# Vision tower on one core: the q, k and v projections as seven products of quarters

## The chip, the cores and the metric

The kernel runs on one core of one Trainium2 chip. The metric is the device time of one execution in microseconds (us). Before the change it is 2117.93 us, the median of three runs from 2116.43 to 2118.93. The engines are named as in the profile: PE multiplies matrices (PEld is its loading of the stationary operand), DVE and ACT work element by element, POOL does small arithmetic and issues indirect transfers, SP issues most of the other transfers.

## The reference

The input x is cut into overlapping patches of 16 samples, each is Fourier transformed, and a matrix W maps the result to tokens of 256 features. On these tokens h stand two residual layers: a retention layer with an MLP, and a mixture of eight experts of which each token uses two.

```python
h = tokens(x) @ W.T
# layer 0, on t = layernorm(h)
a = layernorm(t)
q, k, v = a @ Wq.T + bq, a @ Wk.T + bk, a @ Wv.T + bv
mem = 0
for each token: mem = decay * mem + k * v ; ret = q * mem
t = t + ret
h = h + t + relu(layernorm(t) @ W1.T + b1) @ W2.T + b2
# experts, on u = layernorm(h)
h = h + u + sum over the two chosen e of  weight[e] * (gelu(u @ w1[e] + b1[e]) @ w2[e] + b2[e])
```

There are 16384 tokens, in 32 blocks of 512. All arithmetic that matters here is in 32 bits.

## The kernel before

**Blocks.** The 32 blocks of 512 tokens go through the stages in a software pipeline. In pass `i` of the main loop (0 to 30) the block `new = blocks[i]` is embedded, normalised and sent through q, k, v and the retention scan; `mid = blocks[i-1]` goes through the MLP; `old = blocks[i-2]` is routed to the experts. After the loop the last block (31), the MLP of block 30 and the remaining expert tiles are done in an order written out by hand.

**Expert tiles.** A routed token is written by an indirect transfer to a buffer `xbuf` in its expert's rows. Whenever 256 rows of an expert are full they make a *tile*: `load` fetches weights, rows (turned by the transfer) and shares; `turn` joins the halves on ACT; `enter` does the first product and the Gelu; `leave` the second product; `sums` scales the result on DVE and adds it to the output by an indirect transfer. `slot()` fits one tile step into the pass if more than three tiles are in hand; there are four slots in a pass: after the embedding, after the fourth MLP product group, ahead of the first half of `mlp_out` and ahead of its second half. `take` finds with some twenty small DVE operations which tiles became full.

**Order of work.** The instruction streams of PE, DVE, ACT and SP keep the order of the program (`manual_schedule`); POOL's are placed by the framework. In each pass the order on PE is: five embedding products (L378), a slot, the first MLP layer `mlp_in` (eight groups, L321 with `w_sb`) with a slot after the fourth, the router products `logits` (L583), q, k, v for both halves of the features (L321 with `wqkv_sb`), the counting products of `place` (L653), a slot, `mlp_out(0)` (L517), the transposes of `residual` (L476), a slot, `mlp_out(1)`.

**q, k, v.** `retention(m)` makes for each half m of the 256 features three products of the 512 tokens by 256 features, each as two accumulated matrix products of 512 columns, in one PSUM bank from the pool `p_mm` (four banks). ACT adds the bias of k, DVE adds that of v and multiplies by k, a scan on DVE runs the memory, and DVE adds q's bias and multiplies. On PE each product in 32 bits is two instructions, so a block has 24 of them.

**Transposition of the features.** For blocks 6 to 30 the normalised tokens `zz` are split by ACT into 16-bit planes, turned by a transfer (`turned<-planes`, issued by SP at L309) and joined by DVE (`features1`, L315, for q, k, v) or by ACT (`features2`, for the MLP). The single buffer `turned` also serves the router's turn of the tokens (`turn3`, joined by DVE in `join3`). For blocks 0 to 5 and 31 PE turns them (L288).

**DVE's order in a pass**, as far as it matters: `retention` and `choose` (the routing, which ends in the tile `both`), `place`, `take`, the tile's `sums`, the add and statistics of `mlp_out(0)`, `residual` with its norm, `sums`, the add and statistics of `mlp_out(1)`, the norm's apply (which waits for POOL's `rstd`), the embedding's combinations, its norms, `sums`, `join3`, `sums`, the first part of the next block's `differences`, the join of hT, the second part.

PSUM has eight banks: four in `p_mm`, three in `p_tm` (embedding, transposes, second products) and one in `p_sm` (router and counting products).

Of the kernel before, what the change touches and what calls it, by code (L numbers as in the profile page):

```python
# [36 lines left out]
def vit_tower_kernel(  # L37
# [24 lines left out]
    G = P // TT  # L62
    BLK = TT * P
    U = TT // 2
    NV = 8
# [25 lines left out]

    p_mm = ctx.enter_context(tc.tile_pool(name="p_mm", bufs=4, space=bass.MemoryType.PSUM))
    p_tm = ctx.enter_context(tc.tile_pool(name="p_tm", bufs=3, space=bass.MemoryType.PSUM))
    p_sm = ctx.enter_context(tc.tile_pool(name="p_sm", bufs=1, space=bass.MemoryType.PSUM))
    ident = const.tile([P, P], F32)
# [56 lines left out]
    wqkv_sb = const.tile([P, 3, KD, D], F32)  # L152
    nc.sync.dma_start(out=wqkv_sb, in_=wqkv.rearrange("w (k p) d -> p w k d", p=P))
    w1_sb = const.tile([P, KD, H], F32)
    nc.sync.dma_start(out=w1_sb, in_=w1.rearrange("(k p) h -> p k h", p=P))
# [57 lines left out]
    def fold(w, g, b, to, room, ps):  # L213
# [21 lines left out]
        for k in range(KD):  # L235
            nc.scalar.mul(w[:, :, k, :], w[:, :, k, :], vec[:, g + k : g + k + 1])

    class Norm:

# [76 lines left out]

    def feature_mm(w, rhs, m):

        ps = p_mm.tile([P, BLK], F32, name="mm")
        for k in range(KD):  # L320
            nc.tensor.matmul(ps, lhsT=w[:, k, ts(m, P)], rhs=rhs[:, k, :], start=k == 0, stop=k == KD - 1)  # L321
        return ps
# [9 lines left out]
    class Block:  # L332
# [93 lines left out]
        def retention(self, m):  # L426

            if m == 0:
                self.kv = one.tile([P, KD, BLK], F32, name="kv")
                self.ret = one.tile([P, KD, BLK], F32, name="ret")  # L430
            ks = two.tile([P, BLK], F32, name="ks")
            at = slice(m, m + 1)

            def tiles_order(a):
                return a.rearrange("p (r w) -> p w r", r=TT)

            def own_order(a):
                return a.rearrange("p (w r) -> p w r", r=TT)

            pk = feature_mm(wqkv_sb[:, 1], self.hT, m)  # L440
            nc.scalar.activation(own_order(ks), tiles_order(pk), AF.Identity, bias=vec[:, BK + m : BK + m + 1])  # L441
            pv = feature_mm(wqkv_sb[:, 2], self.hT, m)
            nc.vector.scalar_tensor_tensor(
                own_order(self.kv[:, m, :]),
                tiles_order(pv),
                vec[:, BV + m : BV + m + 1],
                own_order(ks),
                ALU.add,
                ALU.mult,
            )  # L450
            nc.vector.tensor_tensor_scan(  # L451
                ks,
                vec[:, DEC + m : DEC + m + 1].to_broadcast([P, BLK]),
                self.kv[:, m, :],
                0.0 if self.i % NBLK == 0 else carry[:, at],
                ALU.mult,
                ALU.add,
            )
            nc.vector.tensor_copy(carry[:, at], ks[:, BLK - 1 : BLK])
            pq = feature_mm(wqkv_sb[:, 0], self.hT, m)  # L460
            nc.vector.scalar_tensor_tensor(
                tiles_order(self.ret[:, m, :]),
                tiles_order(pq),
                vec[:, BQ + m : BQ + m + 1],
                own_order(ks),
                ALU.add,
                ALU.mult,
            )

        def residual(self):  # L470
            norm = Norm()
            for u in range(U):
# [7 lines left out]
                for i in range(2):  # L480
                    norm.stats(self.z, 2 * u + i)
            norm.factors_here()
            self.zz = one.tile([P, TT, D], F32, name="zz")
# [19 lines left out]
        def mlp_in(self, m):  # L503
            if m == 0:
                self.aT = one.tile([P, KH, BLK], F32, name="aT")
            ps = feature_mm(w1_sb, self.hT, m)
            nc.scalar.activation(self.aT[:, m, :], ps, AF.Relu, bias=vec[:, MB1 + m : MB1 + m + 1])  # L507

        def mlp_out(self, u, between=None):
            if u == 0:  # L510
                self.norm = Norm()
            ps = p_tm.tile([P, 2, D], F32, name="tm")
            for i in range(2):
                if i and between:
                    between()
                for k in range(KH):
# [10 lines left out]
            if u == U - 1:  # L527
                self.norm.factors_here() if self.i >= NS - 1 else self.norm.factors()
                self.tok = one.tile([P, TT, D], F32, name="tok")
                self.norm.apply(self.tok, self.h)  # L530
                if self.i == NS:
                    nc.vector.tensor_tensor(self.h, self.h, self.tok, ALU.add)
                    return
                mean, rstd = self.norm.mv[:, :, 0], self.norm.rstd[:, 0, :]
                self.by = small.tile([P, 2, TT], F32, name="by")
                nc.vector.tensor_scalar(self.by[:, 0, :], rstd, 1.0, None, ALU.add)
                nc.vector.scalar_tensor_tensor(self.by[:, 1, :], mean, -1.0, rstd, ALU.mult, ALU.mult)

        def store(self):
# [38 lines left out]
        def logits(self):  # L578
            self.lg = p_sm.tile([P, TT, G], F32, name="sm")
            for k in range(KD):  # L580
# [67 lines left out]
        def place(self, at_once=True):  # L648

            oh = self.oh  # L650
            ps = p_sm.tile([P, 2, TT, E], F32, name="sm")
            for i in range(2):
# [62 lines left out]
    def take(n, block, writes):  # L715
# [23 lines left out]
        shape = [P, k, E]  # L739
        past = small.tile([P, KMAX, E], F32, name="past")[:, :k, :]  # L740
        nc.vector.tensor_tensor(
# [272 lines left out]

    def slot(known, load=True):

        if len(tiles) - at["enter"] > LEFT and at["enter"] + 2 <= known:
            expert_step(load=load)

# [6 lines left out]
    with tc.manual_schedule(engines=MANUAL):  # L1026
# [3 lines left out]
        for i in range(NS):  # L1030
# [5 lines left out]
            next(embed)  # L1036
            if at["enter"] == 0:
                advance("turn", 2)
            if i > 1:
# [15 lines left out]
            next(embed, None)  # L1055
            slot(known, load=False)
            if old:
                old.join3()
            for m in range(KH):
                if mid:  # L1060
                    mid.mlp_in(m)
                if m == 1:
                    new.split1()

                    if at["enter"]:
                        advance("load", at["enter"] + AHEAD - 1)
                if m == TT - 1:
                    slot(known)
                if m == KH // 2 and old:
                    old.store()  # L1070
                if m == KH - 3:
                    ahead = blocks[i + 1].differences(xs.pop(i + 1))
                    next(ahead)
                    new.features1()
                    next(ahead)
            if i == NS - 1:
                slot(known)
            if old:
                old.logits()
            for m in range(KD):  # L1080
                new.retention(m)
                if old and m == 0:
                    old.choose()
            if old:
                take(old.i + 1, old, old.place(at_once=False))
                old.scatter(1)
            if i + 2 < NB:
                xs[i + 2] = load_x(i + 2)
            slot(known)
            if old:  # L1090
                old.scatter(2, last_product[0])
            if mid:
                mid.mlp_out(0)
            if old:
                old.scatter(3, last_product[0])
            new.residual()
            slot(known, load=False)
            if old:
                old.scatter(4, last_product[0])
            if at["enter"] == 0:  # L1100

                advance("load", 2)
            if i:
                new.split2()
            if at["enter"]:
                advance("load", at["enter"] + AHEAD - 1)
            if mid:
                mid.mlp_out(1)

# [14 lines left out]
        for m in range(KH):  # L1124
# [5 lines left out]
            if m == KH - 3:  # L1130
                last.features1()
        next(weights)
        old.logits()
# [3 lines left out]
        next(weights)  # L1137
        last.retention(0)
        mid.mlp_out(0)
        next(weights)  # L1140
        take(NS - 1, old, writes)
        next(weights)
        mid.mlp_out(1)
        last.retention(1)
        beside = expert_halves(fetch=False)
        next(beside)
        mid.features3()
        mid.rows()
        advance("leave", at["enter"] - 1)
        mid.logits()  # L1150
        mid.choose()
        run(beside)
        expert_step(fetch=False, sums=False)
        writes = mid.place()
        advance("sums", at["leave"])
        expert_step(fetch=False, sums=False)
        last.residual()
        expert_step(fetch=False, sums=False)
        advance("sums", at["leave"])
        expert_step(fetch=False)  # L1160
        take(NS, mid, writes)
# [17 lines left out]
        del tiles[at["load"] :]  # L1179
        cuts = [0] + [min(len(rest), len(rest) * e // (E - 1) + 0) for e in range(1, E)] + [len(rest)]  # L1180
        for e in range(E):
            tiles.extend(rest[cuts[e] : cuts[e + 1]])
            tiles.append(Expert(e, last))
# [99 lines left out]
```

## Time and profile before

The profiled execution took 2119.29 us, with a span of 2117.5 us from its first to its last instruction and a mean granted PE clock of 0.997.

| group | count | busy us | mean ns |
|---|---|---|---|
| PE, second MLP product, L517, 256 columns | 2048 | 453.3 | 380 |
| PE, first MLP product, L321, 512 columns | 1024 | 450.3 | 592 |
| PE, q, k, v products, L321, 512 columns | 768 | 339.0 | 598 |
| PE, embedding products, L378, 256 columns | 1280 | 282.5 | 379 |
| PE, tile products, L859 and L876, 256 columns | 1048 each | 251.6 and 249.5 | 383 and 381 |
| DVE, h add of the MLP, L524 | 64 | 44.2 | 690 |
| DVE, scan, L451 | 56 | 71.9 | 1284 |
| DVE, ret, L461 | 64 | 70.6 | 1104 |
| ACT, bias of k, L441 | 64 | 44.0 | 687 |
| ACT, Gelu, L867, 256 columns | 262 | 109.5 | 470 |
| ACT, copy of embedding products, L387, 512 columns | 32 | 18.7 | 585 |

The mean of a PE instruction is longer than the step from one to the next, because instructions overlap: busy time by count gives the step. A block's lines in a timeline (start and duration in us, engine, line, operation, output and inputs, and in brackets the idle time ahead of it and what ended it) show the order of the work; DVE, ACT and POOL each do one instruction at a time in order.

### The profile page before, as it was taken

What the parts mean: (1) busy time and instruction counts of PE and PEld (TensorE: products, weight loads), DVE (VectorE), ACT (ScalarE), POOL (GpSimd) and SP (SyncE); (2) the same over time, 40 slices, a digit from 0 to 9 for tenths busy, and PEclk for the clock granted to TensorE, in tenths of its full rate; (3) what the DMA queues carried; (4) which work ended last, traced back from release to release, by engine and by line L of the source; (5) the groups of instructions that cost most, each with busy time, mean ns of one, the idle gap of its engine ahead of it and who ended that gap; (6) DMA issues with size and microseconds to landing.
All of it is one profiled execution on the core that took longest, in us unless ns stands there. A gap on an engine that the chain in (4) does not pass through costs nothing.

```text
span 2117.5 us, 28820 instructions
## 1 busy us (share of the span) xinstructions
PE 2093.3 (99%) x8502; PEld 1478.1 (70%) x8502; DVE 1653.6 (78%) x5176; ACT 832.4 (39%) x1329; POOL 876.4 (41%) x769
## 2 busy tenths in 40 slices
PE   8999999999999999999999999999999999999989
PEld 6666666677776667777666777666677766677766
DVE  7778877878888788888878888787788888777545
ACT  2222334444334444433444433344443334443533
POOL 1122243344444444444434444433444443355444
PEclk9999999999999999999999999999999999999999
DMA  4032256765666776566677657666765666686743
GB/s 142 21 106 81 79 137 129 159 138 134 154 138 143 155 160 132 136 155 132 151 155 163 122 136 160 132 150 155 155 131 138 154 133 153 137 205 161 119 58 50
DMA packets 424510, 283.10 MB, mean 134 GB/s; under 512 B 355104, under 2 KB 391072, under 8 KB 420256
## 3 DMA queue, kind: packets, MB, share of 16 engines
q1 hardware_dynamic: 373424, 208.35, 41.2%
q0 software_dynamic: 49632, 67.39, 17.9%
q10 hardware_dynamic: 1296, 5.52, 0.8%
q8 instruction: 67, 1.10, 0.2%
q14 instruction: 91, 0.75, 0.1%
HBM read 118.36 MB, written 86.52 MB: 97 GB/s over the span
## 4 chain that ended last, share of the span: by engine, by line
PE 94%; DVE 3%; DMA 1%; issue 1%; POOL 0%; ACT 0%; DVEq 0%; POOLq 0%
PE mm L321 35%; PE tm L517 20%; PE tm L378 13%; PE mm L859 10%; PE tm L876 10%; PE tm L476 1%; PE tm L955 1%; PE mm L938 1%; PE sm L583 1%; PE mm L137 1%; PE mm L288 1%; DMA xbuf<-row,to 0%; DMA out<-y,known 0%; DMA out<-y,xg 0%; DVE ks L451 0%
## 5 line engine op out<-in xcount | busy, mean ns | idle before, releaser
L905 POOL DMA_INDIRECT out<-y,xg x226 | 370.1, 1638 | 357.2 <-DVE y L895 167.0
L517 PE MATMUL tm<-w_sb,aT 128*128 128x256 f32 x2048 | 453.3, 380 | 2.9 <-DVE h L524 2.9
L321 PE MATMUL mm<-hT,w_sb 128*128 128x512 f32 x1024 | 450.3, 592 | 0.0
L517 PEld LDWEIGHTS tm<-w_sb,aT 128*128 128x128 f32 x2048 | 389.1, 190 | 56.5 <-DVE h L524 3.4
L676 POOL DMA_INDIRECT xbuf<-row,to x248 | 245.8, 991 | 256.4 <-DVE full L727 175.8
L321 PEld LDWEIGHTS mm<-hT,w_sb 128*128 128x128 f32 x1024 | 194.4, 190 | 216.1 <-issue 203.0
L321 PE MATMUL mm<-hT,wqkv_sb 128*128 128x512 f32 x768 | 339.0, 598 | 0.0
L378 PE MATMUL tm<-wu,xv 128*128 128x256 f32 x1280 | 282.5, 379 | 0.0
L321 PEld LDWEIGHTS mm<-hT,wqkv_sb 128*128 128x128 f32 x768 | 143.9, 191 | 174.7 <-issue 165.5
L378 PEld LDWEIGHTS tm<-wu,xv 128*128 128x128 f32 x1280 | 243.0, 190 | 32.4
L867 ACT ACTIVATE ge<-mm,w 128x256 f32<-128x256 f32 x262 | 109.5, 470 | 385.9 <-issue 338.0
L876 PE MATMUL tm<-w,ge 128*128 128x256 f32 x1048 | 249.5, 381 | 5.7 <-DVE y L893 5.7
L859 PE MATMUL mm<-xT,w 128*128 128x256 f32 x1048 | 251.6, 383 | 2.4 <-ACT xT L852 2.4
L507 ACT ACTIVATE aT<-mm,vec 128x512 f32<-128x512 f32 x256 | 172.1, 684 | 177.6 <-PE mm L321 176.9
L876 PEld LDWEIGHTS tm<-w,ge 128*128 128x128 f32 x1048 | 200.3, 191 | 36.2 <-issue 9.4
L859 PEld LDWEIGHTS mm<-xT,w 128*128 128x128 f32 x1048 | 195.5, 191 | 41.0 <-issue 14.2
L852 ACT COPY xT<-xh 128x512 uint16<-128x512 uint16 x262 | 181.9, 764 | 25.8 <-DMA xh<-xbuf 25.5
L301 ACT COPY planes<-zz 128x1024 uint16<-128x1024 uint16 x100 | 99.6, 1043 | 168.5 <-DVE zz L275 168.5
L266 POOL TENSOR_SCALAR rstd<-mv 128x4 f32<-128x4 f32 x62 | 41.7, 672 | 290.7 <-DVE mv L247 288.8
L893 DVE TENSOR_TENSOR y<-tm,w 128x512 f32<-128x512 f32 x131 | 90.5, 691 | 65.7 <-PE tm L876 60.3
L626 POOL TENSOR_TENSOR ex<-euler,second 128x4 f32<-128x4 f32 x32 | 34.6, 1081 | 241.0 <-DVE second L617 241.0
L441 ACT ACTIVATE ks<-mm,vec 128x512 f32<-128x512 f32 x64 | 44.0, 687 | 214.9 <-PE mm L321 214.9
(179 smaller groups left out, 2387.4 us busy)
## 6 DMA issues: line engine op xcount, KB each, us to landing
w<-in_wex SPq DMA_DIRECT2D x113, 641.5 KB, 5.6
xb<-in_x SPq DMA_DIRECT2D x32, 1040.0 KB, 6.7
out<-h SPq DMA_DIRECT2D x31, 512.0 KB, 4.8
bank<-in_wex ACTq DMA_DIRECT2D x8, 641.5 KB, 7.7
xbuf<-row,to POOLq DMA_INDIRECT x248, 2.6
out<-y,xg POOLq DMA_INDIRECT x226, 5.1
xh<-xbuf SPq DMA_TRANSPOSE x131, 4.7
xg<-xbuf SPq DMA_DIRECT2D x131, 4.0 KB, 3.2
```

Of the source, the lines that this page charges most:

```text
L301: nc.scalar.copy(planes[:, :, i * D : (i + 1) * D], half)
L321: nc.tensor.matmul(ps, lhsT=w[:, k, ts(m, P)], rhs=rhs[:, k, :], start=k == 0, stop=k == KD - 1)
L378: nc.tensor.matmul(ps[:, n, :], lhsT=xv[:, i, j, :], rhs=wu[:, i, j, :], start=j == 0, stop=j == J - 1)
L507: nc.scalar.activation(self.aT[:, m, :], ps, AF.Relu, bias=vec[:, MB1 + m : MB1 + m + 1])
L517: last_product[0] = nc.tensor.matmul(ps[:, i, :], lhsT=self.aT[:, k, ts(u * 2 + i, P)], rhs=w2_sb[:, k, :], start=k == 0, stop=k == KH - 1,)
L676: write = nc.gpsimd.indirect_dma_start(out=xbuf, out_offset=bass.IndirectOffsetOnAxis(ap=self.to[:, c, t : t + 1], axis=0), in_=self.row[: ...
L852: nc.scalar.copy(halves[:, :, :, 1 - i], self.xh[:, i * KD : (i + 1) * KD, :])
L859: nc.tensor.matmul(ps[:, m, :], lhsT=self.w[:, k * D + m * P : k * D + (m + 1) * P], rhs=self.xT[:, k, :], start=k == 0, stop=k == KD - 1,)
L867: nc.scalar.activation(self.ge[:, m, :], ps[:, m, :], AF.Gelu, bias=self.w[:, 5 * D + m : 5 * D + m + 1])
L876: last_product[0] = nc.tensor.matmul(ps[:, c, :], lhsT=self.ge[:, k, ts(c, P)], rhs=w[:, (2 + k) * D : (3 + k) * D], start=k == 0, stop=k ...
L893: nc.vector.tensor_tensor(y, ps, w[:, 4 * D : 5 * D].unsqueeze(1).to_broadcast([P, 2, D]), ALU.add)
L905: add = nc.gpsimd.indirect_dma_start(out=out, out_offset=bass.IndirectOffsetOnAxis(ap=number[:, c, :], axis=0), in_=y[:, c, :], in_offset= ...
```

## The change

The 512 tokens of a block are cut into two halves of columns, and the 256 features and outputs into halves too. A product of two such matrices is eight products of quarters; by a scheme with sums formed beforehand it is done in seven.

- `mix_weights` forms once, in pass 0, four combinations of the weights' quarters on DVE (t1, t2, t4 in a new tile `wqkv_mix`, and one written over the quarter W12).
- `mix_tokens` forms in each pass from 1 on four combinations of the quarters of hT on DVE, right after the join of `features1` and ahead of the second part of `differences`: s1, s2, s4 in the room of `planes`, and one in place.
- `products` makes one projection in four stages: two products into a scratch bank, which ACT copies to both halves of a bank `sums[which]` (so that the further products add to it) and, with a bias, to `p5`; two products added; ACT takes one quarter of the result, and copies one half of the bank to the other; two products added, from which DVE takes two quarters with `p5` added; one product added; ACT takes the last quarter. `qkv` runs the stages of k, v and q in turn, and other work is put between the stages. `scan` does the multiplication of k and v, the scan, and the multiplication by q.
- PSUM: `p_mm` goes from four banks to two, three banks become the fixed `sums`, `p_sm` is gone (its two users take banks of `p_tm`). The first MLP layer uses the three `sums` in turn.
- Order in a pass from 1 on: router products, `choose`, stage one, a tile's turn and `enter`, stage two, `place`, that tile's `leave`, stage three, its `sums` and the next tile's `enter`, stage four, the scans, `mlp_out(0)`, `residual`, that tile's `leave`, `mlp_out(1)`. `take` moves from behind `place` into `mlp_out(1)`, between the statistics and the norm's apply. The slots of a pass thereby count only tiles that were known at its start.
- The loads of the first tiles and their turn are shifted accordingly; `x` of block i+2 is loaded behind the tile's loads; the first slot of a pass is left out while no tile has entered.
- After the loop: the stages of the last block's q, k, v stand around the first half of block 30's `mlp_out` and ahead of the second, its residual is begun earlier and ended later, and the tile steps between are ordered anew. The cut of the last tiles among the experts is written more shortly and gives the same cuts.

```diff
+    def mix_weights():
+        w = wqkv_sb.rearrange("p w k (m q) -> p w k m q", q=P)
+        t1, t2, t4 = [wqkv_mix[:, :, i, :] for i in range(3)]
+        nc.vector.tensor_tensor(t1, w[:, :, 0, 1], w[:, :, 0, 0], ALU.subtract)
+        nc.vector.tensor_tensor(t2, w[:, :, 1, 1], t1, ALU.subtract)
+        nc.vector.tensor_tensor(t4, w[:, :, 1, 0], t2, ALU.subtract)
+        nc.vector.tensor_tensor(w[:, :, 0, 1], w[:, :, 1, 1], w[:, :, 0, 1], ALU.subtract)
...
+        def mix_tokens(self):
+            room = one.tile([P, TT, 2 * D], U16, name="planes").rearrange("p t d -> p (t d)").bitcast(F32)
+            a, b = self.hT[:, 0, :], self.hT[:, 1, :]
+            s1, s2, s4 = self.mix = [room[:, ts(i, HALF)] for i in range(3)]
+            nc.vector.tensor_tensor(s1, a[:, HALF:], b[:, HALF:], ALU.add)
+            nc.vector.tensor_tensor(s2, s1, a[:, :HALF], ALU.subtract)
+            nc.vector.tensor_tensor(a[:, HALF:], a[:, :HALF], a[:, HALF:], ALU.subtract)
+            nc.vector.tensor_tensor(s4, b[:, :HALF], s2, ALU.subtract)
...
+            nc.tensor.matmul(ps[:, 0, :], lhsT=w11, rhs=a[:, :HALF], start=True, stop=True)
+            nc.tensor.matmul(ps[:, 1, :], lhsT=t1, rhs=s1, start=True, stop=True)
+            nc.scalar.copy(g, ps[:, 0:1, :].to_broadcast([P, 2, HALF]))
+            p5 = three.tile([P, HALF], F32, name="p5")
+            biased(p5, ps[:, 1, :], 1)
+            yield
+            add(0, w21, b[:, :HALF])
+            add(1, t2, s2)
+            biased(*half(0), 0)
+            nc.scalar.copy(g[:, 0, :], g[:, 1, :])
+            yield
+            add(0, w22, s4)
+            add(1, w12, a[:, HALF:])
...
+            nc.vector.tensor_tensor(dst, src, also, ALU.add)
+            yield
+            add(1, t4, b[:, HALF:])
+            biased(*half(1), 0)
+            yield
...
+                if old:
+                    old.logits()
                     old.choose()
-            if old:
-                take(old.i + 1, old, old.place(at_once=False))
-                old.scatter(1)
-            if i + 2 < NB:
+                next(qkv)
+                next(qkv)
+                tile_steps = slot_halves(known, sums=False)
+                next(tile_steps, None)
+                next(qkv)
+                if old:
+                    writes = old.place(at_once=False)
+                    old.scatter(1)
+                run(tile_steps)
+                if i + 2 < NB:
+                    xs[i + 2] = load_x(i + 2)
+                if old:
+                    old.scatter(2, last_product[0])
+                next(qkv)
+                advance("sums", at["leave"])
+                later = slot_halves(known, load=False)
+                next(later, None)
+                next(qkv)
+                for m in range(KD):
+                    new.scan(m)
+                mid.mlp_out(0)
...
             if mid:
-                mid.mlp_out(1)
+                mid.mlp_out(1, meanwhile=lambda: old and take(old.i + 1, old, writes))
```

## The prediction

> **What bounds the kernel now.** I read the page's busy times and chain of waits first, then the timelines of PE, DVE and SP over one steady block, then the waits. A timeline line begins with start and duration in us; a bracket holds the idle time before it and what ended it.
>
> ```profile
> PE 2093.3 (99%) x8502; PEld 1478.1 (70%) x8502; DVE 1653.6 (78%) x5176; ACT 832.4 (39%) x1329; POOL 876.4 (41%) x769
> ...
> PE 94%; DVE 3%; DMA 1%; issue 1%; POOL 0%; ACT 0%; DVEq 0%; POOLq 0%
> ```
>
> ```profile
> 966.61 10.57 PE L321 MATMUL mm<-hT,wqkv_sb 128*128 128x512 f32 x24
> ...
> 1028.69 10.57 PE L321 MATMUL mm<-hT,wqkv_sb 128*128 128x512 f32 x24
> ```
>
> PE runs without gaps: from one block's q, k, v products to the next is 62.08 us (966.61 to 1028.69), the same in each of the 24 steps from block 6 to block 30. So fewer products should shorten it, as long as nothing else needs almost 62 us per block. One thing does, and the DVE and SP timelines show it:
>
> ```profile
> 973.49 0.29 DVE L607 STREAM_TRANSPOSE turned_lg<-sm 128x128 f32<-128x128 f32 x1
> ...
> 976.28 0.19 DVE L624 TENSOR_TENSOR both_bfloat<-oh 128x32 bf16<-128x32 f32 x1
> ...
> 982.04 0.16 DVE L721 TENSOR_TENSOR full<-ends,first 128x8 f32<-128x8 f32 x1
> ...
> 987.71 0.69 DVE L524 TENSOR_TENSOR h<-tm,h 128x512 f32<-128x512 f32 x1 [0.42 <-PE tm L517]
> ...
> 1003.73 1.38 DVE L275 TENSOR_SCALAR tok<-h,mv,rstd 128x256 f32<-128x256 f32 x4 [2.88 <-POOL rstd L271]
> ...
> 1025.91 1.47 DVE L315 COPY hT<-turned 128x512 uint16<-128x512 uint16 x4 [0.56 <-DMA turned<-planes]
> ```
>
> ```profile
> 1020.25 3.28 SPq L309 DMA_TRANSPOSE turned<-planes  x1
> ```
>
> This is a loop through all engines. The first MLP half ends on PE; DVE adds it to h (987.71), does the residual, the second half's add, norms (tok at 1003.73) and the next block's embedding; its planes are turned by a DMA (1020.25) that waits for DVE's tokT copies; DVE joins hT by 1027.38, and PE needs it at 1028.69. The slack is 1.31 us here. The engine totals don't show that a second resource is only 2% behind PE.
>
> **The change, part by part.** Products: 24 instructions of 0.434 us (10.41 from 966.61 to 977.02) go, 42 of 256 columns come, at 0.216 us (32 of L517 take 6.90): 9.06, so 1.35 saved per block, 41.8 us over 31 blocks if PE stayed without gaps. Weight loads (190 ns) stay under a 216 ns product.
>
> Follow one steady block from J, the end of the hT join. *DVE:* the four mix_tokens operations are 256 wide; the nearest row (L147, 416 ns) gives s1 at J+0.45 and, overlapped by about 0.1 each, all four at J+1.4. The second part of the differences, still ahead of choose, takes 3.33 (1027.27 to 1030.60): J+4.7. choose takes 2.98 (973.49 to the end of L624): `both` at J+7.6. *PE:* the second product of k needs s1, so it starts at J+0.5; then 0.43, v and q 0.86 each, the tile's enter 1.73 and stage two 2.59 end at J+7.0, and place waits for `both` until J+7.7. Before, 10.41 us of products stood between router products and place; now 7 do, and DVE has four operations more ahead of it. Behind the waiting place stand the tile's leave, stages three and four and the MLP half, and DVE waits for that half. From place: 0.06, leave 1.73, stage three 2.59, the later tile's enter 1.73, stage four 1.30, MLP half 6.91: J+22.0, h add at J+22.2.
>
> *Chain back to J:* from h add to tok was 16.02. Moving take (3.56, 982.04 to 985.60 with its neighbours) behind the second half's statistics fills the 2.88 wait for POOL's rstd and runs 0.68 over, while 0.18 of waiting for PE ahead of that half goes: 16.52. From tok to the joined hT 23.65 (1003.73 to 1027.38). J' = J+62.4. A wait on PE also exposes a weight load: after the 1.97 wait at 1950.96 eight products took 1.84 to the next start against 1.73, +0.1. In the waits view DVE idles 18.4 us for this DMA over 25 blocks, 0.74 on average against 0.56 here, +0.18, which the old slack swallowed. **62.65 per block, +0.57**, 13.7 over 24 steps: the 1.35 is saved and then stands as waits before k's second product and before place.
>
> ```profile
> DVE hT L315 <- DMA turned<-planes: 18.4, 25, 2.2
> ```
>
> ```profile
> 1950.96 1.99 PE L859 MATMUL mm<-xT,w 128*128 128x256 f32 x8 [1.97 <-ACT xT L852]
> ...
> 2035.52 3.75 PE L876 MATMUL tm<-w,ge 128*128 128x256 f32 x8 [5.74 <-DVE y L893]
> ```
>
> A longer wait costs more: after 5.74 us the next eight products took 3.75 in place of 1.89 (and the eight behind them 2.99); after 1.97 they were at full speed. I expect waits near 1 us, so no such cost.
>
> The Trainium skill ("TensorE: Matmul & The Clock Gate", Part 1: The HAM clock gate) says PE falls to half clock after an idle window of about 3.4 us and needs about 3.4 us of work to recover. The two rows agree with a limit between 1.97 and 5.74. By the rule the sum stays, as 1 us is below it; were it crossed once per block, an estimate from that page is 1.7 us more each.
>
> *Taken at nothing, with the cover.* ACT gets per projection a 512 copy (0.585, L387), three biased 256 activations (0.47, L867) and a 256 copy (about 0.42): 7.2 less the two ks rows (1.37), +5.8 per block on an engine busy 39%. The enter covers the first seeds, leave the second, the later enter DVE's sums; seeds are ready some 2 us early. If the tile's xh DMA holds ACT's turn (25.5 us in 25 waits, longest 4.9), the excess shows: 0 to 0.3 per block. A copy from PSUM to PSUM has no row; 0.585 to 0.69 bounds it, off the path. DVE's three sums (0.69 to 0.75), two k-v products and two scan tails with strided reads (0.69 to 1.10, L461) end near J+21.5, ahead of h add at J+22.2; at the upper bounds 0.3 per block is lost. Less p_mm (two banks): k's is read by ACT before enter asks for it; without that enter waits 0.5 us. Router results in p_tm: leave needs that bank after choose's first transpose, about J+5 against J+7.8. x's load moves on SP behind a tile's loads, lands in 6.7 us and is needed 50 us later. POOL's scatters come earlier with place, and the sums' adds with them; rstd then follows the later tile's adds as before. Tiles that take finds at the block's end are loaded one block later; the rule of three left in hand covers it, but it also skips the two last slots of block 5, so two tiles (2 x 3.45 = 6.9) go to the end.
>
> *Blocks 1 to 5:* mix_weights, once, is four 384-wide operations, about 0.55 each between L147 and L353 (683 ns at 512), 2.2 of DVE behind block 0, counted in the bounds. Products -6.75; the waits of 1.35 and 1.58 before mlp_out(1) (PE timeline at 194.05 and 245.91) -2.9; two tiles postponed -6.9; against it no tile work stands between the stages, so DVE's place work (2.31) and three sums hold stage four by about 1.2 in blocks 2 to 5, +4.8, and take exceeds its old 1.48 wait there, +2.7. Together -9 (-14 to -5). *End:* postponed tiles +6.9, last block's products -1.35. PE idles some 10 us after 1938, partly for ACT's xT and y; the reorder with two tiles more as cover may take 3 of it (-8 to +5).
>
> Sum against the 2117.5 us span: -9 + 13.7 + 6.9 - 1.3 - 3 = +7.3. The profiled execution took 2119.29, 1.4 above the 2117.93 median, so I add to the median: **2125 us**, own range 2112 to 2142 (0.4 per block either way is 10, the ends some 5).
>
> **Rivals.** (a) *PE stays dense:* all gain arrives; 2117.9 - 41.8 + 0 to 4 = 2078. For it: PE is 99% busy and DVE idles some 11 us per block. Against: half of that idling lies where the order fixes it (rstd waits, the DMA). It needs the loop two us shorter than I sum it. (b) *Only the hT join holds*, place does not (choose quicker or enough room ahead of it): the period loses the 0.7 to 0.9 at place, 61.8, -0.3 per block: -9 - 7 + 6.9 - 1.3 - 3 = about 2104. (c) *DVE or ACT late as well:* scans past J+22.2, or turns waiting for xh between the seeds; another 0.6 to 1.0 per block, from 0.9 us of extra DVE work in the first third on, 2140 to 2150. (d) *The early blocks gain more than -9*, the steady ones as summed: 2118, no change.
>
> **How the numbers follow.** Forecast with (d) inside it 0.52, (b) 0.20, (a) 0.16, (c) 0.12. Faster or slower starts at 0.2%, 4.2 us, about what a measurement tells: the forecast gives 0.03 faster, 0.14 same, 0.35 slower; (b) 0.18 faster, 0.02 same; (a) 0.16 faster; (c) slower. Faster 0.37, same 0.16, slower 0.47. The range 2084 to 2146 leaves out most of (a) and the far end of (c).
>
> **What would show it.** Right: blocks 7 to 30 some 62.5 us apart, PE waiting about 0.9 us at k's second product for DVE's mix and 0.7 at place for `both`; tok directly behind take without a wait for POOL; tokens' hT join waiting for its DMA as before. Wrong: a period near 60.7 with no PE wait (a); 61.8 with none at place (b); PE waits at stages three and four for ACT's seeds, or h add waiting for scans (c).

## The result, and the profile after

The changed kernel takes 2138.83 us (median of 4 runs, 2135.09 to 2141.64) against 2117.61 for the kernel before beside it (2116.43 to 2118.93): a ratio of 1.0099, 95% interval 1.0081 to 1.0116. It is 1.0% slower. 2125 was forecast, so the direction was right and the size short by 14 us. The profiled execution took 2141.64 us; its span is 2139.9, against 2117.5 before, at a mean granted clock of 0.993 against 0.997. It is the longest of the four, 2.8 us above the median; the profiled execution of before was 1.7 above its own.

The page of the changed kernel, busy times:

```profile
span 2139.9 us, 30460 instructions
...
PE 2080.6 (97%) x9060; PEld 1580.7 (74%) x9060; DVE 1759.5 (82%) x5397; ACT 978.0 (46%) x1732; POOL 893.3 (42%) x769
```

PE is busy 12.7 us less than before and the span is 22.4 longer: the products did become cheaper, and more than that came back as waiting. The waits of PE in the changed kernel (engine and waiting instruction, then what it waits for; us in total, times, longest):

```profile
PE tm L773 <- DVE both_bfloat L744: 15.6, 26, 1.7
PE tm L996 <- DVE y L1013: 6.8, 1, 6.8
...
PE mm L520 <- DVE planes L488: 5.9, 17, 0.5
PE mm L519 <- DVE hT L327: 4.1, 5, 1.4
```

The first, third and fourth are the loop that the forecast followed: `place` waiting for the routing (26 times, 0.6 on average), k's second product waiting for the first token combination, k's first for the join. The second is a single wait at the end. One steady block on PE and on DVE (timelines: start, duration, operation, in brackets the idle time before it and its releaser):

```profile
1026.17 0.70 PE L519 MATMUL mm<-hT,wqkv_sb 128*128 128x256 f32 x2
1026.97 0.70 PE L520 MATMUL mm<-planes,wqkv_mix 128*128 128x256 f32 x2
...
1034.27 0.20 PE L773 MATMUL tm<-both_bfloat,rc 128*128 128x32 bf16 x2 [0.56 <-DVE both_bfloat L744]
1034.32 1.97 PE L996 MATMUL tm<-w,ge 128*128 128x256 f32 x8
```

```profile
962.76 1.47 DVE L327 COPY hT<-turned 128x512 uint16<-128x512 uint16 x4 [1.32 <-DMA turned<-planes]
...
971.87 0.19 DVE L744 TENSOR_TENSOR both_bfloat<-oh 128x32 bf16<-128x32 f32 x1
...
985.21 1.08 DVE L577 TENSOR_TENSOR ret<-ret,ks 128x512 f32<-128x512 f32 x1
986.70 0.69 DVE L637 TENSOR_TENSOR h<-tm,h 128x512 f32<-128x512 f32 x1 [0.40 <-PE tm L630]
...
1002.89 1.37 DVE L287 TENSOR_SCALAR tok<-h,mv,rstd 128x256 f32<-128x256 f32 x4
...
1017.87 1.46 DVE L327 COPY tokT<-turned 128x512 uint16<-128x512 uint16 x4
...
1024.92 1.47 DVE L327 COPY hT<-turned 128x512 uint16<-128x512 uint16 x4 [1.36 <-DMA turned<-planes]
```

On DVE, from one join's end (J = 964.23) `both` is ready at J+7.83, the scans end at J+22.06, the h add starts at J+22.47 after waiting 0.40 for PE, tok follows 16.19 later with no wait for POOL (no bracket), and the next join ends 23.50 after tok: 62.16 us around. On PE the two lines after the wait at `place` are the price of each turn: 1026.17 to 1026.97 is 0.80 where a dense pair takes 0.43, so k's second product starts 0.37 later than it could in a dense row.

Where the 22.4 us of span came in, from the first embedding product of a block to that of the next:

| stretch | before | after | difference | forecast |
|---|---|---|---|---|
| start to block 7 | 377.97 | 369.87 | -8.1 | -9 + 0.6 |
| block 7 to 31, 24 steps | 1489.87 | 1503.70 | +13.8 (62.65 a step) | +13.7 (62.65 a step) |
| of these: 18 steps | 62.08 each | 62.28 each | | |
| of these: blocks 9, 10, 19, 28, 29, 30 | 62.08 each | 63.78 each (to 65.00) | | |
| block 31 to the end | 249.68 | 266.29 | +16.6 | +2.6 |

Of the 8.1 us gained before block 7, 7.7 lie in the one step from block 5 to block 6 (62.10 before, 54.44 after), where the work of the two postponed tiles is missing.

The third kernel that matters is one of the experiments, and it beats both: 2101.4 us, from moving one DVE step.

### The profile page after: what moved, and what is told of

Its sections match the earlier page's. It is cut to its first block, busy times and chain, and to the rows that moved or that the text cites. A ratio compares the mean times of both kernels' runs of the same rounds, so it can differ in the third digit from the quotient of the medians.

```text
span 2139.9 us, 30460 instructions
## 1 busy us (share of the span) xinstructions
PE 2080.6 (97%) x9060; PEld 1580.7 (74%) x9060; DVE 1759.5 (82%) x5397; ACT 978.0 (46%) x1732; POOL 893.3 (42%) x769
## 4 chain that ended last, share of the span: by engine, by line
PE 72%; DVE 16%; DMA 8%; issue 2%; POOL 1%; ACT 0%; SPq 0%; POOLq 0%; DVEq 0%; ACTq 0%
PE tm L630 19%; PE tm L391 12%; PE sums L334 12%; PE tm L996 10%; PE mm L979 8%; DMA turned<-planes 7%; PE sums L504 6%; DVE xv L366 2%; DVE xv L363 2%; DVE hT L327 2%; PE tm L588 1%; DMA out<-y,known 1%; PE tm L1075 1%; PE mm L1058 1%; DMA xh<-xbuf 1%
## 5 line engine op out<-in xcount | busy, mean ns | idle before, releaser
L1025 POOL DMA_INDIRECT out<-y,xg x226 | 386.6, 1711 | 454.6 <-DVE y L1015 258.0
L334 PE MATMUL sums<-hT,w_sb 128*128 128x512 f32 x1024 | 450.2, 592 | 0.0
L334 PEld LDWEIGHTS sums<-hT,w_sb 128*128 128x128 f32 x1024 | 194.1, 190 | 216.4 <-issue 205.2
L996 PE MATMUL tm<-w,ge 128*128 128x256 f32 x1048 | 254.4, 386 | 6.8 <-DVE y L1013 6.8
L979 PEld LDWEIGHTS mm<-xT,w 128*128 128x128 f32 x1048 | 200.1, 191 | 40.8 <-issue 14.5
L620 ACT ACTIVATE aT<-sums,vec 128x512 f32<-128x512 f32 x256 | 171.9, 683 | 117.4 <-PE sums L334 115.7
L996 PEld LDWEIGHTS tm<-w,ge 128*128 128x128 f32 x1048 | 196.1, 191 | 39.0 <-issue 10.5
L504 PE MATMUL sums<-hT,wqkv_sb 128*128 128x256 f32 x372 | 110.7, 379 | 0.0
L258 DVE BATCH_NORM_STATS2 st<-h 128x6 f32<-128x256 f32 x256 | 104.8, 409 | 3.3
L366 DVE TENSOR_TENSOR xv<-xb 128x512 f32<-128x512 f32 x160 | 104.1, 683 | 3.1 <-DMA xb<-in_x 3.1
L327 ACT COPY hT<-turned 128x512 uint16<-128x512 uint16 x100 | 66.2, 762 | 81.4 <-DMA turned<-planes 81.4
```

What stands on the lines that cost most here:

```text
L366: nc.vector.tensor_tensor(to, a, b, ALU.subtract)
L504: nc.tensor.matmul(g[:, n, :], lhsT=lhsT, rhs=rhs, start=False, stop=True, skip_group_check=True)
L979: nc.tensor.matmul(ps[:, m, :], lhsT=self.w[:, k * D + m * P : k * D + (m + 1) * P], rhs=self.xT[:, k, :], start=k == 0, stop=k == KD - 1,)
L996: last_product[0] = nc.tensor.matmul(ps[:, c, :], lhsT=self.ge[:, k, ts(c, P)], rhs=w[:, (2 + k) * D : (3 + k) * D], start=k == 0, stop=k ...
L1025: add = nc.gpsimd.indirect_dma_start(out=out, out_offset=bass.IndirectOffsetOnAxis(ap=number[:, c, :], axis=0), in_=y[:, c, :], in_offset= ...
```

## The experiments

Two theories stood at the outset. The **loop theory** is the forecast's: a loop through DVE, the planes' transfer, PE and back sets the period, and what shortens it brings the products' gain. The **order theory** puts the loss into the new order at the end. For the end two more came up later: the **chain theory** (the adds to the output, one tile after another, set the end) and the **PE theory** (a postponed tile costs its PE time there, as the forecast had it).

### Does one DVE instruction more cost its time?

In each block the two operations that form half of the residual's `z` are done a second time, 0.65 us of DVE, in the kernel before and in the changed one.

```diff
+            for t in range(2):
+                nc.vector.tensor_scalar(
+                    self.z[:, t, :],
+                    self.h[:, t, :],
+                    norm.mv[:, t, 0:1],
+                    norm.rstd[:, 0, t : t + 1],
+                    ALU.subtract,
+                    ALU.mult,
+                )
```

> The kernel before with two of the four operations that make z done twice (0.65 us more on DVE per block, ahead of the join of the tokens). Loop theory: the 1.2 us of slack ahead of q, k, v take it; only the five blocks with less slack show some tenths: 2117 to 2121. Rival (the time follows DVE's total work): 31 x 0.65 = 20 us more, 2138.

> The changed kernel with the same 0.65 us more on DVE per block. Loop theory: every steady block is 0.65 longer, 25 x 0.65 = 16 us: 2155 (2150 to 2160). Rival (the loop is not what bounds): under 5 us more, 2137 to 2143.

Measured: before with the dose 2119.5 (2115.09 to 2125.77, 10 runs; ratio 1.0005, 0.999 to 1.0021), so the slack takes it up. The changed kernel with the dose takes 2154.9 (2151.66 to 2158.07, 4 runs; 1.0164, 1.0138 to 1.0191): +16.1, and 25 turns of 0.65 are 16.2. The profiles say it more exactly. In the kernel before, the 24 steps from block 7 to 31 grow by 0.3 us together. In the changed kernel they grow by 15.7, which is 0.66 each, the stretch ahead of them by 3.5, and the end comes out 6.5 shorter, of which more below; the sum of 16 is thus partly a coincidence, the 0.66 a step is not. The same work is free in the steady blocks of the one and costs all of its time in those of the other. That a path through DVE bounds the changed kernel there is shown.

### Shortening the loop at two places

The first variant moves the second part of `differences` behind `choose`, so that the routing is ready 3 us earlier; the second puts the join of the tokens ahead of the tile's sums on DVE, so that the planes' transfer can start earlier; the third does both.

```diff
                     if i:
                         new.mix_tokens()
-                    next(ahead)
+                    if not old:
+                        next(ahead)
...
                     old.choose()
+                    next(ahead)
```

> The changed kernel with choose ahead of the second part of the differences on DVE. Loop theory (period set by hT join, mix, differences, choose, place, MLP half, norms, embedding, planes' transfer): `both` comes 3.3 us earlier, PE's wait of 0.72 us (0.56 plus its bubble) at place goes, the wait at k's second product stays; steady period 62.2 to about 61.5, blocks 2 to 4 lose another 2 us: 2138.8 - 17 - 2 = 2120 (2114 to 2126). Rival (the half-width products, the seeds by ACT or PE itself take the time; the waits only show where slack is burnt): the wait moves to another place and the time stays at 2136 to 2141.

```diff
-            if at["enter"]:
-                slot(known, load=False)
             if old:
                 old.join3()
+            if at["enter"]:
+                slot(known, load=False)
```

> The changed kernel with the join of the tokens (which frees the buffer of the planes' transfer) ahead of the first slot's sums on DVE. Loop theory: the transfer starts 1.6 us earlier, DVE is free for the hT join 1.36 us earlier; the waits at k's second product and at place both go (0.37 and 0.72), and late transfers are partly absorbed: period about 60.9, 2138.8 - 31 = 2108 (2100 to 2116). Rival (the transfer lands when it lands, held by other traffic, or PE itself is slower): 2130 to 2141.

> Both moves together. Loop theory: the loop falls to some 60 us, below PE's own 60.7, so PE bounds: period 60.75, early blocks 2 us less: 2138.8 - 36 - 2 = 2101 (2094 to 2110), not the sum of the two single gains (48 + 2). Rival (independent costs): 2088 to 2092. Rival (neither matters): 2130 to 2141.

| variant | us (runs) | ratio to before | steady step |
|---|---|---|---|
| choose first | 2119.88 (2116.31 to 2126.08, 10) | 1.0006 (0.9995 to 1.0017) | 61.3 to 61.7, late blocks to 64.9 |
| join first | 2101.38 (2099.99 to 2102.74, 4) | 0.9925 (0.9908 to 0.9941) | 61.07, but 61.35 once and 64.74 in block 30 |
| both | 2104.01 (2101.05 to 2106.48, 4) | 0.9939 (0.9922 to 0.9955) | 61.07, but 63.88 in block 30 |

PE timeline with choose first: the wait at `place` is gone (no bracket), that at k's second product is not (1021.63 to 1022.44 is 0.81):

```profile
1021.63 0.70 PE L519 MATMUL mm<-hT,wqkv_sb 128*128 128x256 f32 x2
1022.44 0.70 PE L520 MATMUL mm<-planes,wqkv_mix 128*128 128x256 f32 x2
...
1029.02 0.20 PE L773 MATMUL tm<-both_bfloat,rc 128*128 128x32 bf16 x2
```

With join first both are gone; 0.54 stays between k's two products. Its DVE timeline, then PE's:

```profile
940.38 1.46 DVE L327 COPY tokT<-turned 128x512 uint16<-128x512 uint16 x4
941.74 0.20 DVE L1008 SCALAR_TENSOR_TENSOR tile_share<-xg,w 128x2 f32<-128x2 f32 x1
...
947.62 1.46 DVE L327 COPY hT<-turned 128x512 uint16<-128x512 uint16 x4
```

```profile
950.26 0.70 PE L519 MATMUL mm<-hT,wqkv_sb 128*128 128x256 f32 x2
950.80 0.59 PE L520 MATMUL mm<-planes,wqkv_mix 128*128 128x256 f32 x2
...
957.27 0.20 PE L773 MATMUL tm<-both_bfloat,rc 128*128 128x32 bf16 x2
```

The tokens' join now stands ahead of the tile's sums (L1008), the planes' transfer starts some 1.6 us earlier against DVE's work, and the features' join at 947.62 has no bracket: it waits for nothing. It ends at 949.08, and PE wants it at 950.26, so the loop has slack again and PE is bound by itself: 61.07 us in nearly every block from 7 to 29, with no wait of PE in the view. In block 30 (64.74) PE waits 2.42 us for DVE's `ks`.

Apart from block 30 the blocks of 63 to 65 us are gone too: the transfer no longer lands late in them. SP's issue of the planes' transfer and DVE's join for block 9, in the changed kernel and then with join first:

```profile
517.69 3.40 SPq L321 DMA_TRANSPOSE turned<-planes  x1
525.07 1.48 DVE L327 COPY hT<-turned 128x512 uint16<-128x512 uint16 x4 [3.20 <-DMA turned<-planes]
```

```profile
514.37 1.69 SPq L321 DMA_TRANSPOSE turned<-planes  x1
520.08 1.46 DVE L327 COPY hT<-turned 128x512 uint16<-128x512 uint16 x4
```

The join starts 7.38 us after the issue in the one, and 5.71 in the other without a wait; of 23 such joins with join first a single one waits, 0.52 us, which is the step of 61.35.

2108 was forecast for join first, and 2101 measured. In the profiles the 24 steps are 34.0 us shorter than in the changed kernel, near the 31 forecast; the end is 8.5 shorter, though nothing was changed there (7.6 with choose first, 8.7 with both). That part is not the loop's, and the section on the end comes back to it. Doing both brings no more than the one, as it must when PE sets the period.

### The tiles left in hand

The rule that keeps three tiles in hand in each pass is what postpones two tiles to the end. Here it keeps two.

```diff
-    LEFT = 3
+    LEFT = 2
```

> The changed kernel with two tiles instead of three kept in hand, so that one tile fewer is put off to the end. Theory that the put-off tiles cost more at the end (adds to the output follow one another there) than they save in block 5: block 5 grows by 3.45, the end shrinks by 3.45 of PE and up to 6.5 of the chain of adds: 2138.8 - 1 to - 4 = 2135 to 2138. Rival (the end's excess comes from its new order alone): 2138 to 2140, the end's length less 3.45 only.

A plain miss: 2361.93 us (2361.25 to 2365.61, 4 runs; 1.1159, 1.114 to 1.1177). The step grew to over 71 us. Of this kernel the PE waits, the ACT timeline and SP's timeline:

```profile
PE sums L334 <- ACT aT L620: 210.6, 26, 9.6
```

```profile
1130.97 1.38 ACT L972 COPY xT<-xh 128x512 uint16<-128x512 uint16 x2 [11.54 <-DMA xh<-xbuf]
```

```profile
1120.54 3.29 SPq L321 DMA_TRANSPOSE turned<-planes  x1
1125.04 0.35 SPq L942 DMA_DIRECT2D w<-in_wex  x1
1126.33 1.27 SPq L949 DMA_TRANSPOSE xh<-xbuf  x1
```

The tile that the slot wants in this pass is loaded only in this pass: SP issues its rows at 1126.33, behind the planes, ACT waits 11.54 us with the tile's turn, and behind that stand the ReLUs that PE waits for, 8.1 us on average. The third tile in hand is the lead time of the loads. Two runs tested that on join first: the load at a pass's end is moved behind `mlp_out(1)`, where the tiles that `take` just found are known, with two tiles in hand and with one.

```diff
-    LEFT = 3
+    LEFT = 2
...
-            if at["enter"]:
-                advance("load", at["enter"] + AHEAD - 1)
             if mid:
                 mid.mlp_out(1, meanwhile=lambda: old and take(old.i + 1, old, writes))
+            if at["enter"]:
+                advance("load", at["enter"] + AHEAD - 1)
```

> The kernel of e2 (join of the tokens first) with two tiles in hand instead of three, and the load at a block's end moved behind mlp_out(1), so behind take. e4 showed rows arriving 11 us late because new tiles were loaded one block later, behind the planes' transfer. If that late load is what cost e4 its 8 us per block: no wait of ACT's turn, steady blocks at 61.1 as in e2, one tile fewer at the end, -6.7 of the chain of adds, +3.45 in block 5: 2101.4 - 3 = 2098 (2094 to 2102). Rival (two in hand are too few anyhow): ACT waits for rows in each block, above 2130.

> As e7 with one tile in hand: the steady passes are the same, since a pass has four slots; block 30's pass takes one tile more, so the end has two tiles fewer than in the changed kernel. Chain of adds bounds the end: another 3 to 6 below e7, 2094 (2088 to 2098), if the end's first tile steps find their rows loaded. Rival: they don't, PE waits some 8 us there, 2100 to 2106.

Measured: 2103.31 us (2102.76 to 2104.01, 4 runs; 0.9931, 0.9915 to 0.9948) and 2108.9 (2094.68 to 2118.72, 10 runs; 0.995, 0.9929 to 0.9972). The step stays at 61.07, so the late load was what made the 71. But neither gains over join first, and both miss what was forecast, 2098 and 2094. Their last stretch, from block 31's embedding, takes 260.0 and 271.5 us against 257.9, with the adds of 29 tiles in it instead of 30: PE waits there for tiles in the making (7.1 us in one wait with two in hand, 9.8 with one). The second kernel's times spread over 24 us, with the slowest in the profile, and decide little.

### The end: order, or the chain of adds?

The changed kernel with the order of before behind the loop (the last block's q, k, v and residual, and the tile steps between):

```diff
-        out_steps = mid.mlp_out_steps(0)
-        next(out_steps)
...
-        run(out_steps)
+        mid.mlp_out(0)
...
-        expert_step()
+        mid.mlp_out(1)
+        next(qkv)
...
```

> The changed kernel with the last block's stages of q, k, v, its residual and the tile steps beside them in the places where the kernel before has its two retention halves and residual (stages one and two ahead of mlp_out(0), three and four behind mlp_out(1)). Theory that the end is long because of two more tiles, whose adds to the output go one after another, some 6.5 to 7 us each: the order hardly matters, 2135 to 2142. Rival (the new order is what makes the end 16.6 us longer): 2122 to 2132.

2141.56 us (2140.72 to 2142.15, 4 runs; 1.0101, 1.0079 to 1.0124). The order isn't the loss. In the end's last 100 to 150 us each tile is finished by two adds to the output. POOL's timeline of the changed kernel at the end:

```profile
2119.90 1.54 POOL L1025 DMA_INDIRECT out<-y,known  x1 [3.01 <-DMA out<-y,known]
2121.75 1.64 POOL L1025 DMA_INDIRECT out<-y,known  x1 [0.30 <-issue]
2126.33 1.54 POOL L1025 DMA_INDIRECT out<-y,known  x1 [2.94 <-DMA out<-y,known]
2128.18 1.54 POOL L1025 DMA_INDIRECT out<-y,known  x1 [0.30 <-issue]
2132.44 1.58 POOL L1025 DMA_INDIRECT out<-y,known  x1 [2.72 <-DVE zz L1083]
```

Two adds of 1.54 with 0.30 between them, then some 3 us for the transfers to land before the next tile's adds may start: 6.4 and 6.1 us per tile here. The last bracket names DVE, whose work was long done; the pitch shows that it is the same wait. From some 100 us behind the start of block 31 on, the pitch is 6.9 us on average, before as well as after; PE needs 3.45 per tile. The profiler's duration of such an add is its issue alone. This agrees with the Trainium skill ("Perfetto Trace Analysis", DMA Instruction — SWDGE (GPSIMD)), which says that the reported end is that of writing the descriptors, not of moving the data. From block 31's embedding on, 28 tiles were added before and 30 after. So the chain theory prices the two tiles at 13.8, the PE theory at 6.9.

To test it, the adds of two tiles at the end are left out, with all of their other work kept (512 routed rows are missing from the output):

```diff
-            for c in range(2):
+            for c in range(0 if at["sums"] in (113, 115) else 2):
```

> The changed kernel without the adds to the output of two tiles of the last 30 (their products, Gelu and scaling stay, four indirect transfers are left out, so 512 routed rows are missing in the output). Theory that the chain of adds bounds the end: it is 13 to 14 us shorter, until PE (whose last product ends 9 us before the span's end) bounds again; with PE's wait of 6.8 us for POOL also gone: 2125 to 2130. Rival (PE's 6.9 us for two more tiles is the whole cost): 2136 to 2141.

2128.42 us (2125.36 to 2133.65, 7 runs; 1.004, 1.0024 to 1.0056): 10.4 us less, with not one product less on PE (in the profiles the end is 14.9 shorter, and PE's wait of 6.8 is gone). The chain of adds bounds the end. Then the other way, two tiles more at the end, in the kernel before and in join first, both with `LEFT = 5`:

```diff
-    LEFT = 3
+    LEFT = 5
```

> The kernel before with five tiles left in hand in place of three: two tiles' work moves from the blocks (where PE is dense) to the end. Chain theory (at the end each further tile costs one step of the chain of adds to the output, about 6.9 us by the adds of the kernel before, while PE gets 3.45 back per tile earlier): 2 x (6.9 - 3.45) = +7, so 2124 to 2126 from 2118. PE theory (a postponed tile costs its PE time at the end, as the prediction had it): 0, so 2118. The end, from the last block's embedding on, should grow by 13.8 by the first and by 6.9 by the second.

> As the join-first version, with five tiles left in hand in place of three. Chain theory: its end grows by 2 x 6.6 = 13.2, its early blocks shorten by 6.9: 2101.4 + 6.3 = 2108 (2105 to 2111). PE theory: 2101.4.

| kernel | us (runs) | ratio to before | stretch before block 31 | end |
|---|---|---|---|---|
| before, five in hand | 2123.44 (2118.3 to 2127.13, 11) | 1.0025 (1.0015 to 1.0034) | -5.2 | +10.1 |
| join first, five in hand | 2111.93 (2110.25 to 2115.5, 10) | 0.9973 (0.9964 to 0.9983) | -4.8 against join first | +16.8 against join first |

The PE theory expected no change in either, and both are slower, by 5 and by 10.5. A tile more at the end cost 5.0 and 8.4 us, a tile's adds less saved 5.2: all above PE's 3.45, around the chain's 6.9. For the first, the end was expected to grow by 13.8 on the chain theory and by 6.9 on the PE theory, and 10.1 lies halfway.

The profiles show what blurs this: the pace of the adds differs from one profile to another. Single steps lie between 6.1 and 9.3 us before and after; the mean over the last tiles is 6.68 with five in hand against 6.90 in the kernel before, and 6.71 against 6.63 in join first. Over the 21 and 23 steps of the kernels compared that is some 4 us for the one and 2 against the other, so at equal pace both pairs would have cost about 15 (an estimate from these means), near the chain's price. The same holds for the ends that became shorter without a change behind the loop: with choose first, join first, both, and the dose in the changed kernel the end takes 257.7 to 259.9 us in place of 266.3, with the same 30 tiles, and the adds 6.60 to 6.72 apart in place of 6.89. What sets the pace isn't settled.

## Why the forecast was right, and where it was short

**The steady blocks: right.** 62.65 us per step was forecast, 62.65 measured. `both` at J+7.6 was J+7.83, the h add at J+22.2 was J+22.47, from there to tok 16.52 was 16.19, from tok to the join 23.65 was 23.50. Tok stands directly behind `take`, the join waits for its transfer, `place` waits 0.6 on average (forecast 0.7). The sum hits exactly partly by two errors of opposite sign: the loop alone is 62.16, 0.24 shorter than summed, and the late transfers cost more than their 0.18 per block. That part was luck. Six blocks stand 1.5 us above the other eighteen, 0.37 spread over 24: in five the transfer lands late, in block 30 PE waits for ACT's Gelu instead.

**k's second product: 0.37 late, not 0.9.** PE itself is busy for longer than forecast. Join first shows it without waits: 61.07, so the products save 1.01 per block and not the 1.35 that 42 of 0.216 against 24 of 0.434 gave. The 0.34 that PE takes more, and the loop's 0.24 less, shorten this wait. Rival (a), PE dense, would have been worth 24 us over these steps rather than 32.

**No clock cost of waits near 1 us: wrong in two blocks, 9 and 28.** The PE timeline of block 9 in the changed kernel, and a window over its products (width, busy time and count of PE, PEld, DVE, ACT, POOL, granted clock, share of the DMA engines, GB/s):

```profile
525.91 0.70 PE L519 MATMUL mm<-hT,wqkv_sb 128*128 128x256 f32 x2 [1.38 <-DVE hT L327]
527.13 0.91 PE L520 MATMUL mm<-planes,wqkv_mix 128*128 128x256 f32 x2 [0.52 <-DVE planes L488]
527.84 1.06 PE L519 MATMUL mm<-hT,wqkv_sb 128*128 128x256 f32 x2
```

```profile
527.00:531.00 4.00, 3.87 (x10) 3.09 (x11) 3.90 (x9) 1.92 (x4) 2.32 (x2) 0.57 0.73 181
```

The planes' transfer took 1.8 us longer than in a usual block, PE waited 1.38 and 0.52, and behind that the clock was 0.57 for 4 us: five pairs of products from 527.13 to 531.08 took 3.95 us where 2.2 are usual. The 1.7 us that the forecast named as the price of such a fall is about what this cost. This block costs 2.7 us over the usual 62.28. Block 28, with 1.14 and 0.53, costs 2.5; blocks 10 and 29, with 0.6 and 0.5, keep their speed and cost 1.0. The forecast had priced the waits one at a time.

**Start and early blocks: right in sum.** -8.1 against -8.4; the two postponed tiles, forecast at 6.9, are the step that is 7.7 shorter.

**ACT's seeds, the scans, POOL's scatters: rightly taken at nothing,** though the scans end only 0.4 ahead of the h add; rival (c) was that near.

**The end: the mis-sized term.** "*End:* postponed tiles +6.9, last block's products -1.35. PE idles some 10 us after 1938, partly for ACT's xT and y; the reorder with two tiles more as cover may take 3 of it (-8 to +5)." It measured +16.6 in place of +2.6. This step of the forecast failed. It priced the tiles in PE's time, in a stretch where PE was not what ended last; the adds' pitch puts them at 2 x 6.9 = 13.8. With that chain setting the end, neither the 1.35 saved on PE nor the cover for PE's idle time can bring anything; PE's idle time there grew, from 9.2 to 12.6. By this price the tiles make 13.8 of the 16.6; the other 2.8 aren't attributed, and between profiles the end of the same instructions differs by some 8 us, most of it the pace of the adds. That much was to be had from the profile of before. POOL's timeline, and one line of DVE's:

```profile
2022.36 1.54 POOL L905 DMA_INDIRECT out<-y,known  x1 [4.42 <-DMA out<-y,known]
2024.21 1.55 POOL L905 DMA_INDIRECT out<-y,known  x1 [0.30 <-issue]
2028.67 1.54 POOL L905 DMA_INDIRECT out<-y,known  x1 [2.92 <-DMA out<-y,known]
2030.52 1.55 POOL L905 DMA_INDIRECT out<-y,known  x1 [0.30 <-issue]
2031.51 1.64 POOL L626 TENSOR_TENSOR ex<-euler,second 128x4 f32<-128x4 f32 x1
```

```profile
2033.18 0.17 DVE L631 TENSOR_SCALAR share<-ex 128x4 f32<-128x4 f32 x1 [10.06 <-POOL ex L626]
```

The adds show the same pitch, and PE's longest wait, 5.74 for `y`, was read for its clock and not for what held DVE. What held it is POOL's power for the expert weights (`ex`), queued behind the adds: DVE waits 10.06 us for it there and 9.48 in the changed kernel, and PE's wait of 6.8 above stands behind that.

## What to carry to other kernels

When the busiest engine has no gaps, look for the loop through the other engines that is only just shorter, and price a saving by that loop's slack: 1.3 us of slack in 62 turned a saving of 1 us in each block into a loss until one join was moved ahead of work that could come later. Price work that is put off to the end in the pitch of the resource that ends the program, not in the time of the engine that was busy where it came from. And a dose of extra work, 0.65 us that one kernel absorbs and the other pays in full, tells in one run whether that engine's order bounds it.

## What the runs showed of the hardware that was not expected

- **Two short waits close together were followed by a slower PE.** Behind 1.38 and 0.52 us with one pair of products between them the clock was 0.57; behind 1.14 and 0.53 in block 28 it was 0.66 from 1716 to 1720, and choose first is slow in the same two blocks (0.65 behind 1.30 and 0.52). Behind 0.6 and 0.5, or a single wait of 1.97 in the kernel before, the products kept their speed. No run varies the waits alone. The Trainium skill ("TensorE: Matmul & The Clock Gate", Part 1: The HAM clock gate) gives an activity window of about 3.4 us that runs freely and after which an idle PE falls to half clock. No wait here lasted that long; the number that disagrees is 1.9 us of waiting in 2.6.
- **Adds to the output go at 6.1 to 9.3 us per tile** of two transfers, 6.9 on average, of which POOL's two issues are 3.1.
- **A copy from PSUM to PSUM on ACT** takes about as long as one to SBUF (0.57 to 0.61 against 0.585 for 512 columns, L387 before). ACT timeline of the changed kernel:

```profile
1027.77 0.57 ACT L521 COPY sums<-mm 128x512 f32<-128x512 f32 x1 [1.37 <-PE mm L520]
...
1028.62 0.60 ACT L521 COPY sums<-mm 128x512 f32<-128x512 f32 x1
...
1032.89 0.36 ACT L528 COPY sums<-sums 128x256 f32<-128x256 f32 x1
```

The bracket on the first line is ACT waiting for k's late product.

- **The planes' transfer** lets the join start 5.4 to 5.8 us after its issue in 18 of the 23 blocks from 8 to 30, and 7.38 and 7.12 in the two slow ones. What it met there isn't settled. In the kernel before it was as late as 7.28 once, which the slack took up; with join first it is not late in these blocks.
